# Expert weights kept on chip in the tail of a convolution, attention and expert kernel, with token numbers in buffers of their own

## The chip, the cores and the metric

The kernel runs on one core of a Trainium2 chip. The metric is the device time of one execution in microseconds (us); less is better. A profiled execution gives the trace from which all the rows below are taken.

A core has five engines that run side by side, each through its own instructions in order: TensorE (PE, with its weight loads as PEld), VectorE (DVE), ScalarE (ACT), GpSimd (POOL) and SyncE (SP). SP and POOL mostly start DMA transfers here; sixteen DMA engines carry them out.

## The reference, cut to what matters

```python
# layer 0: 32 convolution paths (1x1, 3x3, 1x1, each with batch norm and relu), summed
x = relu(paths.sum(axis=0) + x)                       # (8, 56, 56, 256)
# layer 1: attention without softmax, then a mixture of experts
t = to_tokens(x)                                      # 8 images of 3136 tokens of 256 numbers
t = t + attention(layernorm(t))                       # per head: q (k^T v) / N, plus its input
tokens = layernorm(t)
probs = softmax(tokens @ router_w.T)                  # 8 experts
rw, re = top_k(probs, 2); rw = rw / rw.sum()
out = tokens
for e in range(8):
    h = gelu(tokens @ w1[e] + b1[e])
    out = out + combine[:, e:e + 1] * (h @ w2[e] + b2[e])
t = t + out
```

Each token goes through two experts only: its first choice and its second choice. All is in 32-bit floating point.

## The kernel before

The tokens of the 8 images form 56 chunks of 448 tokens (7 per image). The main loop (L1542) runs over 65 slots. In a slot the convolution of one chunk is worked on beside the attention of the chunk eight slots back, the routing of earlier chunks, and a number of expert tiles. The convolution's last slot is 56. Slots 57 to 64 have attention (chunks 49 to 55), routing and expert tiles; after the loop, L1604 issues the expert tiles that are left. "The tail" below is everything from slot 57 on.

**Routing.** For a chunk, VectorE works out both choices of each token and its place in the expert's list. POOL then scatters each token's row (256 numbers, two weights, the token's number) into a table in memory, `regions[0]` for first choices and `regions[1]` for second choices: eight indirect DMAs per chunk (`scatter`, L1162). When a round of chunks is closed (`closing`, L548; in the last image after its chunks 1, 3, 5 and 6), `plan_steps` (L1189) makes a table on the chip that lists full tiles of 256 rows: for each tile its first row and its expert. The tiles of a round are numbered first choices before second choices. There are 210 tiles in all. The last round holds tiles 176 to 209; 30 of these start in rows that belong partly to other tiles (`low` is not None), and of such a tile only the rows from `low` on are added.

**One tile.** `take_rows` (L1350) reads the tile's first row into a register of SP and starts the load of 256 rows (259 KB) into `z`, one of 8 buffers. `take_weights` (L1361) reads the expert's number into a register of SP and starts the load of that expert's weights (513 KB) from `Wd`, a table in memory, into `w`, one of 4 buffers. `tile_in` (L1369) transposes the rows on TensorE (`te`), ScalarE copies them to `eT`. `tile_mid` multiplies by the first matrix (`ph`, L1415), ScalarE applies gelu (`hT`, L1419). `tile_out` multiplies by the second (`py`, L1431 and L1435), ScalarE scales by the token's weight into `y` (L1439), one of 4 buffers. `tile_add` (L1444) lets POOL add `y` to the rows of the output in memory: two indirect DMAs per tile (L1453), each for 128 tokens, whose token numbers are read from `z` itself, or for the partial tiles from a small tile `index` that VectorE makes (L1386 and L1387).

**Order.** In block n (`moe_steps`, L1473) stand, one after the other: `tile_in(n)`, first half of `tile_mid(n-1)`, second half and `take_rows(n+2)`, first half of `tile_out(n-2)` and `take_weights(n+1)`, second half of `tile_out(n-2)`. With the first two goes a `tile_add`. Slots 57 to 64 get 45 such blocks; the rest follows after the loop. The order on TensorE, ScalarE and VectorE is written out by hand, with places in the slot (`places`); SP's and POOL's instructions are ordered by the framework. The list `apart` is filled in slot 57 (L1599); from then on the two halves of `ph` and of `py` have separate PSUM banks.

**Waits around the change.** A row buffer is free for a later tile when its last reader is done: the scaling on ScalarE (the weights stand in `z`), and, where the token numbers are read from `z`, the scatter-add's landing. A `y` buffer is free when the scatter-adds of that tile have landed. `ordered_sum` (L1461) lets each scatter-add of a (round, choice) group wait until all those of the group before have landed, because a token has one row in each group. The row loads of a round wait for all `regions` scatters and for the writes of the output's base values by chunk (`out_dram<-X`, L1034) of that round (`before`, in `entry`, L1325).

Of the kernel before, what the change touches and what calls it, by code (L numbers as in the profile page):

```python
# [8 lines left out]
F32 = mybir.dt.float32  # L9
BF16 = mybir.dt.bfloat16  # L10
I32 = mybir.dt.int32
# [14 lines left out]
def kernel(  # L26
# [24 lines left out]
    nc = tc.nc  # L51
    B, N, C = x.shape
# [3 lines left out]
    E = w1.shape[0]  # L56
    HC = 32
    NH = C // HC
    P = 128
# [32 lines left out]
            tc.add_manual_dep(ins, halved[0].name, SYNC, reason="not needed by the first chunk")  # L92
        xs_in[s] = X

    xtp = ctx.enter_context(tc.tile_pool(name="xtp", bufs=4))
    taps = ctx.enter_context(tc.tile_pool(name="taps", bufs=1))
    split = ctx.enter_context(tc.tile_pool(name="split", bufs=1))
    hlp = ctx.enter_context(tc.tile_pool(name="hlp", bufs=2))
    setup_pool = tc.tile_pool(name="setup", bufs=1)
    setup = setup_pool.__enter__()  # L100

# [9 lines left out]
    for g in range(NG):  # L111
        nc.scalar.dma_start(
            out=bn2s[32 * g : 32 * g + 32],
            in_=bn2[32 * g : 32 * g + 32].rearrange("(a e) k -> e a k", a=4),
# [117 lines left out]
    for dx in range(3):  # L232
        for g in range(NG):
            nc.gpsimd.dma_start(
                out=W2s[dx : 3 * 32 : 3, g],
                in_=W2[32 * g : 32 * g + 32].rearrange(
                    "q (dy dx o) -> dx q dy o", dy=3, dx=3
                )[dx],
# [218 lines left out]
    slots = ctx.enter_context(tc.tile_pool(name="slots", bufs=4))  # L457
# [43 lines left out]
    ROW = C + 3  # L501
    WROW = 2 * NF * C + NF
# [5 lines left out]
    def paced(ins):  # L508

        tc.add_manual_dep(ins, pace[0].name, SYNC, reason="spread over the slot")  # L510
        return ins
# [17 lines left out]
    Wd = tc.dram_tile([E, P, WROW], F32, name="Wd")  # L529
# [44 lines left out]
    for e in range(M):  # L574
# [5 lines left out]
        out=below, in_=below, compare_op=ALU.is_ge, fill=0.0, base=-1,  # L580
# [8 lines left out]
        out=earlier, in_=earlier, compare_op=ALU.is_ge, fill=0.0, base=-1,  # L589
# [14 lines left out]
    def unordered(ins, group, keep=()):  # L604

        tc.declare_no_dep(ins, group=group, keep=keep, reason="other rows")
# [715 lines left out]
    got, weights_of, turned, hidden, ready = {}, {}, {}, {}, []  # L1322
    landed = set()

    def entry(i, j, most):  # L1325

        place, own, k, partial, b = slot_of[i]
        loads, (value,) = nc.values_load_multi_w_load_instructions(
            place[0:1, j : j + 1], engines=[mybir.EngineType.SP],
            min_val=0, max_val=most,  # L1330
            skip_runtime_bounds_check_because="a tile's row and expert, made on the chip",
        )
        if b not in landed:
            landed.add(b)
            for ins in before[b]:
                tc.add_manual_dep(loads[0].ins, ins.name, SYNC, reason="rows of the tiles")
        return value

    def empty_rows(e):
        pad = slots.tile([P, 2, ROW], F32, tag="rows", name=f"pad_{e}", bufs=8)  # L1340
        nc.gpsimd.memset(pad, 0.0)
        for k in range(2):
            ins = nc.sync.dma_start(
                out=regions[k][e * CAPR : e * CAPR + TR, :].rearrange("(h p) c -> p h c", p=P),
                in_=pad,
            ).ins
            paced(ins)
            filled(0, ins)

    def take_rows(i):  # L1350
        row = entry(i, 0, E * CAPR - TR)
        z = slots.tile([P, 2, ROW], F32, tag="rows", name=f"rows_{i}", bufs=8)
        region = regions[slot_of[i][2]]
        ins = nc.sync.dma_start(
            out=z, in_=region[bass.ds(row, TR), :].rearrange("(h p) c -> p h c", p=P)
        ).ins
        unordered(ins, "rows")
        tc.add_to_no_dep_group("tiles", ins)
        got[i] = z

    def take_weights(i):  # L1361
        e = entry(i, 1, E - 1)
        w = slots.tile([P, WROW], F32, tag="w", name=f"w_{i}")
        nc.sync.dma_start(
            out=w, in_=Wd[bass.ds(e, 1), :, :].rearrange("e p c -> (e p) c")
        )
        weights_of[i] = w

    def tile_in(i):  # L1369
        z = got.pop(i)  # L1370
        k = slot_of[i][2]
        tp = ps_mm.tile([P, NF, TR], F32, tag="mm", name=f"te_{i}")
        for f in range(NF):
            for h in range(2):
                nc.tensor.transpose(  # L1375
                    tp[:, f, h * P : (h + 1) * P], z[:, h, f * P : (f + 1) * P], ident
                )
        eT = work.tile([P, NF, TR], F32, tag="eT", name=f"eT_{i}")
        nc.scalar.copy(eT, tp)
        g = z[:, :, C + k]  # L1380
        index = [z[:, h, C + 2 :].bitcast(I32) for h in range(2)]
        low = slot_of[i][3]
        if low is not None:
            index = slots.tile([P, 2], I32, tag="index", name=f"index_{i}", bufs=12)
            past = slots.tile([P, 2], I32, tag="past", name=f"past_{i}", bufs=2)
            nc.vector.tensor_scalar(past, pos, low, float(1 << 30), ALU.is_lt, ALU.mult)  # L1386
            nc.vector.tensor_tensor(  # L1387
                index, z[:, :, C + 2].bitcast(I32), past, ALU.bitwise_or
            )
            index = [index[:, h : h + 1] for h in range(2)]  # L1390
        turned[i] = (eT, g, index)

    apart = []
# [29 lines left out]
    def tile_out(i, h):  # L1423
# [15 lines left out]
        nc.scalar.activation(y[:, h, :], ps, AF.Identity, scale=g[:, h : h + 1])  # L1439
        ready.append((i, h))  # L1440

    blocks = {}

    def tile_add():  # L1444
# [97 lines left out]
    for s in range(S + A + 1):  # L1542
        a = s - A
        work_of = []
        era = " alone" if s < A else ""
        if s <= S:
            work_of.append((0.0, 1.0 if is_chunk(s) else 0.1, conv3_steps(s)))
        if is_chunk(s + 2):
            work_of.extend(at("conv1" + era, conv1_steps(s + 2)))
        if is_chunk(s + 1):  # L1550
            work_of.extend(at("taps" + era, [(0.0, lambda: spread_taps(s + 1))]))
            work_of.extend(at("conv2" + era, conv2_steps(s + 1)))
        if is_chunk(s - 1):
            if s < S:
                work_of.extend(at("end" + era, end_steps(s - 1)))
            else:
                work_of.append((0.12, 0.99, end_steps(s - 1)))
        if is_chunk(a + 1):
            work_of.extend(at("fetch", [(0.0, lambda: fetch(a + 1))]))
        if is_chunk(a):  # L1560
            opens = a % NCH == 0
            if opens:
                work_of.extend(at("image", image_steps(a // NCH)))
            if a + A > S:
                work_of.extend(at("attention first last" if opens else "attention last", attn_steps(a)))
            else:
                work_of.extend(at("attention first" if opens else "attention", attn_steps(a)))
        work_of.extend(left)
        left = []
        group = waiting  # L1570
        if waiting and put_off(waiting[0]):
            group = [] if waiting[0] == a - 1 else waiting[:1]
        if group and (len(group) == 2 or group[-1] % NCH == NCH - 1):
            last_image = group[-1] >= S - NCH
            compute, scatters = route_steps(group)
            rt = places["route" if s < S else "route last"]
            work_of.append((rt[0], rt[1], compute))
            if last_image:
                work_of.append((places["scatter last"][0], 0.995, sum(scatters, [])))
            else:  # L1580
                work_of.append((places["scatter"][0], 0.995, scatters[0]))
                left = [(0.0, places["scatter"][1], steps) for steps in scatters[1:]]
            if group[-1] in closing:
                work_of.append((places["plan"][0], places["plan"][1], plan_steps(closing.index(group[-1]))))
            waiting = waiting[len(group) :]
        while r + 1 < len(closing) and known_in[r + 1] <= s:
            r += 1
        if r >= 0 and r + 1 < len(closing):
            goal = upto + (known_after[r] - 2 - upto) // (known_in[r + 1] - s)
            if r + 2 < len(closing):  # L1590
                goal = min(known_after[r] - 2, goal if s < known_in[1] else tiles_by(s))
            work_of.append((places["tiles"][s <= known_in[r]], places["tiles"][2], moe_steps(upto, goal)))
            upto = goal
        if s == 1:
            center_router()
        if 1 <= s <= E:
            work_of.append((0.5, 0.5, [(0.0, lambda: copy_weights(s - 1))]))
            work_of.append((0.8, 0.8, [(0.0, lambda: empty_rows(s - 1))]))
        if s == S + 1:  # L1599
            apart.append(s)  # L1600
        issue(*work_of)
        if is_chunk(a):
            waiting.append(a)
# [60 lines left out]
```

## Time and profile before

| | |
|---|---|
| time, median of 3 runs | 3093.45 us (3087.57 to 3095.67) |
| time of the profiled execution | 3092.02 us |
| its span in the trace | 3090.3 us |
| PE busy | 2875.4 us (93%) |
| DVE busy | 2124.4 us (69%) |
| ACT busy | 1920.2 us (62%) |
| POOL busy | 1800.1 us (58%) |
| loads `w<-Wd` | 210, 513.0 KB each |
| loads `rows<-regions` | 210, 259.0 KB each |
| scatter-adds of `y` (L1453) | 420, in two forms (token numbers from `rows` or from `index`) |

"Busy" is the time in which the engine had an instruction under way; DMA-issuing instructions count only for POOL's indirect DMAs. The rows of the trace read: start, duration, engine, line, operation, output `<-` inputs, shapes; in square brackets how long the engine was idle before and what by the trace released it. Where an instruction waits for several things, the trace names the one that came last by its own account, which can be one that had long been done. In the page's strip of forty slices, the last eight cover the tail and the two slots before it:

```profile
PE   7999898888999999999999999999999997997798
DVE  6877778788777777787777777787778784544000
POOL 2332344445465765756766666576664556676677
DMA  3534344436456777677776776767766666998897
```

Each digit is the busy share of a slice of 77 us in tenths. VectorE has little to do in the tail, POOL and the DMA engines more than before.

### The profile page before, as it was taken

The numbers are of one execution on the slowest core, as the hardware profiler recorded it, in microseconds if no ns is written. First come the engines' busy times: TensorE is split into PE (matmuls) and PEld (weight loads), VectorE is DVE, ScalarE is ACT, GpSimd is POOL, SyncE is SP. The second block draws the span as 40 slices with busy tenths as digits, with TensorE's granted clock in tenths as the row PEclk, the third lists the DMA queues.
The fourth block names the chain that finished last, engine by engine and source line by source line (L and its number), as shares of the span: only waits on it lengthen the run. The fifth ranks groups of instructions, "written<-read, shape, count | busy, mean of one in ns | idle before, by whom it ended". The sixth has DMA issues, their size and how long they took to land.

```text
span 3090.3 us, 53454 instructions
## 1 busy us (share of the span) xinstructions
PE 2875.4 (93%) x16677; PEld 1645.2 (53%) x16677; DVE 2124.4 (69%) x5532; ACT 1920.2 (62%) x3859; POOL 1800.1 (58%) x1333
## 2 busy tenths in 40 slices
PE   7999898888999999999999999999999997997798
PEld 3334443433455555555555555555555554776687
DVE  6877778788777777787777777787778784544000
ACT  4666566556666666667766666666666764554355
POOL 2332344445465765756766666576664556676677
PEclk8999999889999999999999999999999999998899
DMA  3534344436456777677776776767766666998897
GB/s 101 151 118 129 115 141 134 129 98 198 140 158 185 186 193 188 177 198 190 193 193 164 197 197 171 200 168 199 198 171 175 184 169 157 228 254 201 201 236 172
DMA packets 321708, 537.53 MB, mean 174 GB/s; under 512 B 40192, under 2 KB 231824, under 8 KB 321424
## 3 DMA queue, kind: packets, MB, share of 16 engines
q1 hardware_dynamic: 238464, 429.89, 45.6%
q0 software_dynamic: 82368, 103.47, 18.6%
q8 instruction: 133, 2.18, 0.3%
q14 instruction: 151, 1.24, 0.1%
q10 hardware_dynamic: 592, 0.76, 0.1%
HBM read 248.01 MB, written 192.55 MB: 143 GB/s over the span
## 4 chain that ended last, share of the span: by engine, by line
PE 72%; DVE 8%; ACT 6%; POOL 5%; DMA 5%; issue 4%; SPq 0%; ACTq 0%; POOLq 0%; DVEq 0%
PE c L660 14%; PE su L681 13%; PE ph L1415 11%; PE py L1435 9%; PE at L983 7%; PE kv L829 3%; PE c L324 3%; ACT r L665 3%; POOL hsd L793 3%; PE te L1375 3%; PE c L288 2%; DVE r L668 2%; PE py L1431 2%; DMA w<-Wd 2%; DMA out_dram<-y,rows 2%
## 5 line engine op out<-in xcount | busy, mean ns | idle before, releaser
L668 DVE SCALAR_TENSOR_TENSOR r<-c,nb,r 128x448 f32<-128x448 f32 x1792 | 1128.3, 677 | 401.2 <-ACT r L665 395.5
L665 ACT ACTIVATE r<-c,b3t 128x448 f32<-128x448 f32 x1792 | 1036.6, 634 | 342.6 <-PE c L660 338.1
L1453 POOL DMA_INDIRECT out_dram<-y,rows x360 | 567.0, 1575 | 415.6 <-ACT y L1439 262.8
L660 PE MATMUL c<-hl,W3hl 64*128 64x448 f32 x3584 | 684.9, 427 | 32.5 <-ACT r L665 18.7
L1163 POOL DMA_INDIRECT regions<-pay,rrowi x448 | 428.5, 957 | 308.9 <-PE c L660 172.8
L660 PEld LDWEIGHTS c<-hl,W3hl 64*128 64x128 f32 x3584 | 324.3, 188 | 490.6 <-issue 207.7
L681 PE MATMUL su<-r,gather 128*32 128x448 f32 x3584 | 532.2, 564 | 36.3 <-DVE r L668 32.5
L1415 PE MATMUL ph<-eT,w 128*128 128x256 f32 x1680 | 454.5, 402 | 40.2 <-DMA w<-Wd 24.0
L1439 ACT ACTIVATE y<-py,rows 128x256 f32<-128x256 f32 x420 | 196.9, 473 | 442.0 <-PE py L1435 364.9
L1435 PE MATMUL py<-w,hT 128*128 128x256 f32 x1680 | 432.8, 382 | 0.0
L1415 PEld LDWEIGHTS ph<-eT,w 128*128 128x128 f32 x1680 | 301.2, 194 | 173.0 <-issue 45.8
L793 POOL TENSOR_TENSOR hsd<-hsd,half 112x36 f32<-112x36 f32 x49 | 302.7, 6178 | 88.0 <-DVE hsd L791 84.1
L754 POOL TENSOR_TENSOR norm<-t,hmean 112x512 f32<-112x512 f32 x112 | 115.5, 1057 | 361.0 <-DVE hmean L743 220.9
L1419 ACT ACTIVATE hT<-ph,w 128x256 f32<-128x256 f32 x420 | 198.1, 476 | 187.7 <-PE ph L1415 130.9
L1435 PEld LDWEIGHTS py<-w,hT 128*128 128x128 f32 x1680 | 292.1, 192 | 29.3
L983 PE MATMUL at<-tab,tT 128*112 128x272 f32 x896 | 258.2, 411 | 7.1 <-ACT r L665 5.9
L681 PEld LDWEIGHTS su<-r,gather 128*32 128x32 f32 x3584 | 97.2, 109 | 218.7 <-issue 101.7
L1431 PE MATMUL py<-b2hl,own 128*128 128x256 f32 x420 | 182.2, 434 | 11.6 <-ACT lg L991 7.8
L983 PEld LDWEIGHTS at<-tab,tT 128*112 128x112 f32 x896 | 148.3, 179 | 81.5 <-issue 27.7
L987 DVE SCALAR_TENSOR_TENSOR X<-at,rs,X 112x256 f32<-112x256 f32 x224 | 107.0, 478 | 107.2 <-PE at L983 106.6
L1431 PEld LDWEIGHTS py<-b2hl,own 128*128 128x128 f32 x420 | 80.5, 192 | 141.8 <-issue 48.0
L324 PE MATMUL c<-R,W2t 96*32 96x448 f32 x1344 | 149.3, 546 | 0.1
(263 smaller groups left out, 3063.1 us busy)
## 6 DMA issues: line engine op xcount, KB each, us to landing
w<-Wd SPq DMA_DIRECT2D x210, 513.0 KB
rows<-regions SPq DMA_DIRECT2D x210, 259.0 KB
xi<-in_x_dram SPq DMA_DIRECT2D x56, 448.0 KB
hl<-hi SPq DMA_DIRECT2D x112, 224.0 KB
tTs<-xT SPq DMA_DIRECT2D x56, 448.0 KB
ts<-t SPq DMA_DIRECT2D x56, 448.0 KB
tT<-tTs SPq DMA_DIRECT2D x56, 448.0 KB
X<-ts SPq DMA_DIRECT2D x56, 448.0 KB
```

The lines of the kernel that those rows point to most:

```text
L324: nc.tensor.matmul(ps[0][32 * g : 32 * g + 32, :CH], W2t[:, g, dy, :], R[:, g, :].rearrange("q (r w) -> q r w", w=W58)[:, dy : dy + ROWS, ...
L660: product = nc.tensor.matmul(tiles[g][:, :CH], W3hl[rows, ab, cg, :], hl[rows, ab, :], start=True, stop=True)
L665: nc.scalar.activation(r, tiles[0][:, :CH], AF.Relu, bias=b3t[:, cg, 2 * ab : 2 * ab + 1])
L668: nc.vector.scalar_tensor_tensor(r, tiles[1][:, :CH], nb3[:, cg, 2 * ab + 1 : 2 * ab + 2], r, op0=ALU.max, op1=ALU.add,)
L681: nc.tensor.matmul(ps[32 * c4 : 32 * c4 + 32, :CH], gather, unit.pop((s, 4 * u + c4)), start=(ab == 0), stop=(ab == NQ - 1),)
L793: nc.gpsimd.tensor_tensor(sd, sd, half[:T, :].rearrange("q (k h) -> q k h", k=KT), ALU.pow)
L983: nc.tensor.matmul(ps, tT[:, f, k * T : (k + 1) * T], tables_of[b][:, f, :], start=(f == 0), stop=(f == NF - 1),)
L1163: ins = nc.gpsimd.indirect_dma_start(out=regions[n], out_offset=bass.IndirectOffsetOnAxis(ap=v["row_i"][:, (m - group[0]) * KT + k, n : n ...
L1415: nc.tensor.matmul(ps, w[:, f * C + hf * P : f * C + (hf + 1) * P], eT[:, f, :], start=(f == 0), stop=(f == NF - 1),)
L1431: nc.tensor.matmul(ps, own.to_broadcast([P, P]), b2hl, start=True, stop=False)
L1435: nc.tensor.matmul(ps, hT[:, f, h * P : (h + 1) * P], w[:, (NF + f) * C : (NF + f + 1) * C], start=False, stop=(f == NF - 1),)
L1453: ins = nc.gpsimd.indirect_dma_start(out=out_rows, out_offset=at, in_=y[:, h, :], in_offset=None, compute_op=ALU.add, **partial,).ins
```

## The change

The convolution's four pools of buffers move to the other side of the on-chip memory and are closed at slot 57. In their place one tile `experts` (128 partitions, 8 experts, 1026 numbers each) is made there, and one DMA on SP's queue loads all weights into it. From slot 57 on, `take_weights` no longer loads from memory: VectorE reads the expert's number into a register and copies that expert's part of `experts` into `w`. Also from slot 57 on, the token numbers of the tiles that are not partial are copied by VectorE into an `index` tile; there are 20 such tiles instead of 12. The row buffers are 7 instead of 8, from the start of the kernel.

```diff
-    xtp = ctx.enter_context(tc.tile_pool(name="xtp", bufs=4))
-    taps = ctx.enter_context(tc.tile_pool(name="taps", bufs=1))
-    split = ctx.enter_context(tc.tile_pool(name="split", bufs=1))
-    hlp = ctx.enter_context(tc.tile_pool(name="hlp", bufs=2))
+    conv_pools = [
+        tc.tile_pool(name=name, bufs=bufs, side="right")
+        for name, bufs in (("xtp", 4), ("taps", 1), ("split", 1), ("hlp", 2))
+    ]
+    xtp, taps, split, hlp = (p.__enter__() for p in conv_pools)
...
-    def entry(i, j, most):
+    def entry(i, j, most, engine=mybir.EngineType.SP):
...
-            place[0:1, j : j + 1], engines=[mybir.EngineType.SP],
+            place[0:1, j : j + 1], engines=[engine],
...
-        if b not in landed:
+        if b not in landed and engine == mybir.EngineType.SP:
...
-        z = slots.tile([P, 2, ROW], F32, tag="rows", name=f"rows_{i}", bufs=8)
+        z = slots.tile([P, 2, ROW], F32, tag="rows", name=f"rows_{i}", bufs=7)
...
     def take_weights(i):
+        w = slots.tile([P, WROW], F32, tag="w", name=f"w_{i}")
+        if apart:
+            e = entry(i, 1, E - 1, mybir.EngineType.DVE)
+            nc.vector.tensor_copy(
+                w, experts[0][:, bass.ds(e, 1), :].rearrange("q e c -> q (e c)")
+            )
+            weights_of[i] = w
+            return
         e = entry(i, 1, E - 1)
-        w = slots.tile([P, WROW], F32, tag="w", name=f"w_{i}")
...
-        if low is not None:
-            index = slots.tile([P, 2], I32, tag="index", name=f"index_{i}", bufs=12)
+        if apart and low is None:
+            index = slots.tile([P, 2], I32, tag="index", name=f"index_{i}", bufs=20)
+            nc.vector.tensor_copy(index, z[:, :, C + 2].bitcast(I32))
+            index = [index[:, h : h + 1] for h in range(2)]
+        elif low is not None:
+            index = slots.tile([P, 2], I32, tag="index", name=f"index_{i}", bufs=20)
...
         if s == S + 1:
+            for pool in reversed(conv_pools):
+                pool.__exit__(None, None, None)
+            stay = ctx.enter_context(tc.tile_pool(name="stay", bufs=1, side="right"))
+            experts.append(stay.tile([P, E, WROW], F32, name="experts"))
+            nc.sync.dma_start(out=experts[0], in_=Wd.rearrange("e p c -> p e c"))
             apart.append(s)
```

More of the change, by code (lines that the diff above doesn't have):

```diff
@@ L1339, in empty_rows @@
     def empty_rows(e):
-        pad = slots.tile([P, 2, ROW], F32, tag="rows", name=f"pad_{e}", bufs=8)
+        pad = slots.tile([P, 2, ROW], F32, tag="rows", name=f"pad_{e}", bufs=7)
         nc.gpsimd.memset(pad, 0.0)
@@ L1440, in tile_out @@
         ready.append((i, h))
+    experts = []
     blocks = {}
```

## Prediction

> **What bounds the kernel now.** I read the table by stretches first, because the change acts only in the last slots of the loop. The columns are the stretch, its length, busy time of PE, PEld, DVE, ACT and POOL with instruction counts, the granted clock, the DMA share and GB/s.
>
> ```profile
> 2641.00:2697.00 56.00, 53.47 (x284) 45.91 (x283) 29.78 (x134) 29.72 (x71) 36.33 (x27) 0.97 0.97 243
> 2697.00:2887.00 190.00, 157.24 (x792) 133.70 (x791) 75.91 (x347) 90.75 (x217) 138.74 (x111) 0.91 0.87 224
> 2887.00:2955.00 68.00, 59.17 (x287) 49.87 (x286) 1.69 (x10) 29.86 (x66) 41.37 (x28) 0.95 0.89 205
> 2955.00:3090.00 135.00, 122.59 (x647) 107.85 (x646) 8.21 (x49) 72.03 (x148) 104.47 (x68) 0.97 0.82 202
> ```
>
> TensorE looks like the bound and the DMA engines nearly full. The waits of the tail (from 2450 us, engines and SP's queue) seem to confirm that weights and row buffers come late:
>
> ```profile
> ACT y L1439 <- DMA out_dram<-y,rows: 54.8, 13, 12.2
> PE ph L1415 <- DMA w<-Wd: 24.0, 16, 3.6
> PE te L1375 <- DMA rows<-regions: 8.6, 4, 7.5
> SPq L1354 <- DMA out_dram<-y,rows: 163.0, 42, 13.4
> SPq L1364 <- PE py L1435: 121.6, 45, 10.0
> ```
>
> The largest engine wait of these is not for weights: ScalarE waits to write `y` until an older scatter-add of `y` has landed. So I read POOL's instructions in order of time. POOL issues two scatter-adds per tile (L1453) and eight `regions` scatters per chunk (L1163):
>
> ```profile
> 2744.25 1.55 POOL L1453 DMA_INDIRECT out_dram<-y,rows  x1 [0.30 <-ACT X L1025]
> 2746.10 1.55 POOL L1453 DMA_INDIRECT out_dram<-y,rows  x1 [0.30 <-issue]
> 2754.82 1.54 POOL L1453 DMA_INDIRECT out_dram<-y,rows  x1 [7.17 <-DMA out_dram<-X]
> 2908.20 1.54 POOL L1453 DMA_INDIRECT out_dram<-y,rows  x1 [0.30 <-issue]
> 2915.90 1.54 POOL L1453 DMA_INDIRECT out_dram<-y,rows  x1 [6.16 <-ACT hT L1419]
> 3015.50 1.54 POOL L1453 DMA_INDIRECT out_dram<-y,index  x1 [0.30 <-issue]
> 3021.39 1.56 POOL L1453 DMA_INDIRECT out_dram<-y,rows  x1 [4.34 <-ACT y L1439]
> ```
>
> One scatter-add takes 1.55 plus 0.30, so 1.85 us, or 3.70 per tile; one `regions` scatter 0.94 plus 0.30, so 1.25. From 2696 to the last scatter at 3083.22 POOL has no gap above 0.8 us except eight. They fall just at `ordered_sum`'s borders (L1461): the first scatter of one (round, choice) group waits until the whole group before has landed. Counting back from tile 209, the gaps stand before tiles 144, 149, 154, 165, 168, 172, 176 and 193, which are group borders; the borders at 158 and 162 are covered by `regions` scatters. The releasers named in brackets had long been done. Start to start, the eight are 8.72, 7.69, 6.90, 5.34, 7.70, 6.16, 6.57 and 5.89 us: 54.97 us, of which 8 x 1.85 would pass anyway. The borders cost 40.2 us.
>
> So POOL's queue carries the tail. TensorE runs ahead until the four `y` buffers stop it, and its waits for `w` lie inside that lead. In the last stretch both are close: TensorE needs 4.13 us per tile (one group of eight `ph` matmuls to the next in the chain: 3037.46 to 3041.59), POOL 3.70. Only from 2641 to 2697 is POOL waiting for tiles, and there TensorE has 53.5 busy of 56 us and no wait for `w`.
>
> **What the skill says.** The Trainium skill, "SBUF — State Buffer", section "Who interferes with whom": a VectorE copy in a two-port mode and a GpSimd instruction exclude each other, the later one blocks. "VectorE: DVE Perf Modes", section "What auto-detection actually checks": a single-source instruction with both sides in SBUF gets such a mode. The new weight copy is one. The trace agrees only in part. `hi` (L340, 128x448, 394 ns) is such a copy by its speed; it met a scatter-add already running at 961, 1298 and 2417 us, and these took 1.61 to 1.62 us instead of 1.54 to 1.60, while `hi` itself took 0.59 once. But an instruction with two SBUF inputs that had begun 0.16 us ahead of POOL's held it up for 0.5 us:
>
> ```profile
> 2856.49 0.76 DVE L1270 TENSOR_TENSOR big<-iot,qi 128x578 f32<-128x578 f32 x1
> 2856.65 2.07 POOL L1453 DMA_INDIRECT out_dram<-y,rows  x1 [0.30 <-issue]
> ```
>
> "DMA: Bandwidth & Descriptors", section "Queues, rings and completion order": each DMA engine takes turns between the queues that have packets. So scatter packets share engines with the weight packets. The landing times of L1453 agree: median 5.4 us from 2690 to 3090, and 2.7 from 3066 on, once the loads have stopped:
>
> ```profile
> DMA to landing us min/median/max: 2.7/5.4/8.9
> DMA to landing us min/median/max: 2.7/2.7/2.7
> ```
>
> **The change part by part.**
>
> *Weight loads leave SP and the DMA engines.* From slot 57 (about 2641 us, the first tile whose halves have banks of their own) 81 tiles follow, so some 81 loads of 513 KB go: 41.6 MB. In the stretch 2697 to 2887 SP issues 29 of them, 15.2 MB of 42.6 MB (224 GB/s x 190 us), so 36% of the bytes; where only tiles run it is half (513 KB beside 259 of rows and 256 of scatter-adds). The 24.0 us of `ph` waiting for `w` go as well, but they lie in TensorE's lead over POOL: late next is the scatter-add's landing that frees `y`, and behind it POOL. I count them at nothing. If POOL were not the cover they would be worth 24 us.
>
> *Faster landings.* At the eight borders POOL waits for a landing and nothing else. Of their mean interval of 6.87 us I take 0.9 for the restart (an estimate, the trace does not part the two), so the landing is 6.0, inside the 2.7 to 8.9 of the view. The floor is 2.7. With 36 to 50% of the bytes away I let half of the excess of 3.3 go: 1.65 us each, 13.2 us in all. Bounds: 0 if scatter packets hinder themselves, 26 if landings reach the floor.
>
> *A VectorE copy per tile.* 128x1026 elements. From `hi`: 394 ns for 448; at two elements a cycle of 0.96 GHz (the skill's clock, page "VectorE: DVE Perf Modes") 233 ns of it is streaming, 160 fixed, so 1026 take 0.69 us; at one element a cycle 1.23. Ahead of it stands one load of the expert's number into a register: SP's L1328 shows 278 ns, while the skill ("DMA: Bandwidth & Descriptors", "Latency and other measured facts") gives a floor near 600 ns; I take 0.3 to 0.6. With the index copy (0.16, as L1387) VectorE gets some 1.4 us per tile, 63 us for the 45 tiles of slots 57 to 64, in which it is busy 107 of 314 us. There is room. The copy waits for the buffer that tile n-3 leaves, one block back in TensorE's order, and behind it stand attention's VectorE operations, which need later matmuls anyway; who waits for those is ScalarE's normalisation and then POOL's `regions`, which lag. Cost in VectorE time: none.
>
> *The copy against POOL.* POOL starts an instruction every 1.85 us. A copy of 0.69 us in progress at such a start delays it by what is left of it, less 0.09 (the 0.76 us instruction above had 0.60 left and cost 0.52). With random phase that is 0.60 x 0.60 / (2 x 1.85), so 0.097 us per tile. Between tile 137 and 175 POOL is the bound: 39 x 0.097, 3.8 us lost. Behind that TensorE's 4.13 against 3.70 takes it up. Bounds: 0, and, if the phase is locked badly, 0.6 a tile.
>
> *The index copy and seven row buffers.* With its own index buffer a row tile is free after ScalarE has scaled `y`, no longer after the scatter has landed. SP's 163 us at L1354 mostly go. This takes no work from POOL, so by itself nothing; what is late next is `y`, which still waits for the scatter. Seven instead of eight row buffers act earlier too, before slot 57: there SP waited at L1354 only 5.1 us (168.1 in the whole run, 163.0 after 2450), since a tile takes 6 us or more; 0 to 2 us, taken as 0.
>
> *The load of all weights.* 4.2 MB on SP's queue, after the last reader of the convolution's tiles (the last load into `tTs` is issued at 2584.93, its transposes follow). At the 243 GB/s of the next stretch it needs 17 us, and later loads queue behind it. Between 2600 and 2641 it is covered by the tiles of slot 56; if it were issued only at 2641, the first copies would wait up to 10 us for it, in the stretch where POOL has no backlog. I take 0, range 0 to 10.
>
> Sum: -13.2 + 3.8 = -9.4 us. The span of 3090.3 becomes 3080.9, and the profiled run of 3092.02 becomes 3082.6. That run lies 1.4 below the median of 3093.45; from the median I forecast 3084.
>
> **The rivals.**
>
> *POOL bound, gain kept* (the forecast): 3070 to 3092. For it: a POOL queue without gaps but at borders. Chance 0.50.
>
> *The gain is eaten:* the load of all weights is late (+10), or landings hardly shorten because rows, attention and the scatters themselves fill the engines (saving 0 to 4). Time 3092. For it: windows with a DMA share of 0.60 (700 to 1000 us) still show a median landing of 4.6. Chance 0.20.
>
> *Weights are the bound after all,* as the chain of waits suggests, which names `w<-Wd` again and again between 2727 and 2971: then the waits of `ph` (24.0) and `te` (8.6) both go, 33 us, giving 3061. Against it: ScalarE stood at `y`, not at `hT`, for the longer time. Chance 0.09.
>
> *Slower:* the copy holds POOL's starts. Place: every tile from 137 on, 73 tiles. Price: up to 0.6 us a tile when the phase is locked (the copy is released by matmuls that wait for `y`, which waits for a scatter). It decides from 13.2/73, so 0.18 us a tile. With 0.45 it is 33 us against 13 saved: 3113. Chance 0.21.
>
> **How the numbers follow.** A change under 0.3% (9.3 us) cannot be told from none here. Of the forecast's 0.50 some 0.38 lie beyond that, 0.12 within. Faster: 0.38 + 0.09 = 0.47. Same: 0.12 + 0.18 = 0.30. Slower: 0.02 + 0.21 = 0.23. The forecast's own range is 3070 to 3092; the range for all goes from 3064 (near the floor of landings) to 3108 (0.38 us a tile).
>
> **What would show it.** Right: POOL's order still without gaps in the tail, its eight border intervals near 5.2 us; landings of L1453 near 4; no `w` wait at `ph`, yet ScalarE still waiting for `y`; scatter-adds of up to 2.1 us now and then. Wrong: POOL idle for want of `y`, so that TensorE sets the end; scatter-adds at 1.9 us in the mean; TensorE standing still near 2650 for the weights' load; or another order of POOL's scatters that uncovers the borders at 158 and 162 or covers others.

## The result and the profile after

The changed kernel takes 3102.02 us (median of 7 runs, 3097.27 to 3105.78), the kernel before 3095.67 in the runs beside it (3086.28 to 3101.12). The ratio is 1.0024, with a 95% interval of 1.0014 to 1.0033: slower by a quarter of a per cent. The interval leaves out "no change", though the step is smaller than the 0.3% named in the prediction. The profiled execution took 3103.07 us, its span is 3101.2, so 10.9 more than the 3090.3 of the profile before.

The table by stretches of the changed kernel, with the columns of the prediction's first table:

```profile
2641.00:2697.00 56.00, 50.65 (x264) 43.13 (x265) 33.73 (x139) 26.92 (x64) 34.86 (x26) 0.97 0.74 152
2697.00:2887.00 190.00, 160.86 (x821) 136.58 (x820) 92.91 (x398) 90.77 (x224) 141.26 (x108) 0.92 0.70 145
2887.00:2955.00 68.00, 56.62 (x270) 45.91 (x269) 21.81 (x61) 25.92 (x64) 47.85 (x31) 0.95 0.64 103
2955.00:3101.00 146.00, 124.78 (x655) 109.02 (x653) 27.02 (x79) 62.72 (x151) 113.12 (x69) 0.94 0.51 84
```

The last two columns, the share of the DMA engines and the GB/s, fell as they should: 0.87 to 0.70 and 224 to 145 between 2697 and 2887. The scatter-adds' packets land sooner too. Their time to landing from 2690 on (minimum, median, maximum), where before the median was 5.4:

```profile
DMA to landing us min/median/max: 2.7/3.8/5.7
```

So the change did to the transfers what it says, and the kernel is slower all the same. The waits from 2450 on, of the engines and of SP's queue:

```profile
ACT y L1451 <- DMA out_dram<-y,index: 162.1, 51, 12.4
DVE w L1366 <- PE py L1447: 147.1, 42, 12.8
SPq L1355 <- ACT y L1451: 244.9, 66, 10.6
```

No wait of `ph` for `w` is left (24.0 us before), and SP's row loads now wait for ScalarE's scaling, not for landed scatters. ScalarE's wait for a landed scatter-add before it writes `y` has grown to 162.1 us, from 56.9 in both forms (54.8 and 2.1). POOL carries the tail more than before, so the next thing to read is POOL's order of time, here in the last stretch:

```profile
2991.03 1.54 POOL L1466 DMA_INDIRECT out_dram<-y,index  x1 [0.30 <-ACT hT L1431]
2992.88 1.97 POOL L1466 DMA_INDIRECT out_dram<-y,index  x1 [0.30 <-issue]
2995.16 1.54 POOL L1466 DMA_INDIRECT out_dram<-y,index  x1 [0.30 <-ACT eT L1387]
2997.01 1.97 POOL L1466 DMA_INDIRECT out_dram<-y,index  x1 [0.30 <-issue]
2999.29 1.54 POOL L1466 DMA_INDIRECT out_dram<-y,index  x1 [0.30 <-ACT y L1451]
3001.14 1.98 POOL L1466 DMA_INDIRECT out_dram<-y,index  x1 [0.30 <-issue]
```

Every second scatter-add takes 1.97 instead of 1.54 us. VectorE's order of the same microseconds shows what goes with it:

```profile
2992.75 0.70 DVE L1366 COPY w<-experts 128x1026 f32 x1 [3.10 <-PE py L1447]
2996.87 0.70 DVE L1366 COPY w<-experts 128x1026 f32 x1 [3.10 <-PE py L1447]
3001.00 0.70 DVE L1366 COPY w<-experts 128x1026 f32 x1 [3.10 <-PE py L1447]
```

Each weight copy starts some 0.14 us before a scatter-add, and that scatter-add is 0.43 us longer. The phase is locked: the two keep the same distance from tile to tile, and the numbers fit one reason for it. TensorE releases the copies, and it runs here at its own 4.13 us per tile: between 2970 and 3055 its matmuls wait 0.2 us in all. POOL by itself would need 3.70 per tile, so its starts move up on the copies by 0.43 us a tile. But the earlier in a copy a scatter-add begins, the longer it is held. The two settle where the hold is just 4.13 - 3.70 = 0.43 us. Of the 15 tiles 184 to 198, 12 pay 0.43 or 0.44 us, and the 15 together 6.1. At tile 199 the copy comes 0.02 us after the scatter-add's start, doesn't hold it, and the lock is lost. As long as it lasts, POOL, the faster of the two, is bound to TensorE's pace and no longer works off what it is behind. The run without index copies, below, locks again at the same price: 0.43 or 0.44 us for each of the tiles 183 to 192 and 198 to 204. The waits between 2970 and 3065 say the same. Before the change:

```profile
ACT y L1439 <- PE py L1435: 22.0, 44, 0.5
ACT y L1439 <- DMA out_dram<-y,index: 1.3, 1, 1.3
```

and after it:

```profile
ACT y L1451 <- DMA out_dram<-y,index: 41.1, 20, 3.9
```

Before, ScalarE waited there for TensorE, since POOL had caught up; now it waits for landed scatters to write `y`. TensorE's last `te` is at 3069.88 before and at 3071.55 after, so TensorE lost 1.7 us over the whole run; the last scatter-add ends 14.9 us behind it before and 24.1 us after.

An account of POOL's queue, summed from the trace, runs from the first scatter-add of tile 135 to the end of the last one. In each kernel it is 150 scatter-adds and 56 `regions` scatters, 345.1 us at 1.54 and 0.94 us with 0.30 between them. "Lengthening" is what the instructions take above 1.54 or 0.94; "borders" is what POOL stands idle above 0.30 before the group borders. The last column is the time from the first routing matmul (`rk`) of slot 57 to tile 135's first scatter-add. Ratios are to the kernel before, with 95% intervals; the seven variants are those of the experiments below.

| kernel | ratio | POOL in all | lengthening | borders | slot 57 |
|---|---|---|---|---|---|
| before | 1 | 390.5 | 3.3 | 40.2 | 53.5 |
| before, a second profile | | 388.5 | 2.8 | 39.1 | 53.3 |
| after | 1.0024 (1.0014 to 1.0033) | 398.1 | 18.6 | 33.4 | 56.2 |
| copy issued twice | 1.0053 (1.0039 to 1.0068) | 401.0 | 24.4 | 28.9 | 59.1 |
| without index copies | 1.0018 (1.0011 to 1.0026) | 393.6 | 18.7 | 28.8 | 56.2 |
| index copies alone | 0.9979 (0.9971 to 0.9987) | 384.6 | 2.8 | 35.1 | 53.4 |
| weights by a reduction | 0.9972 (0.9960 to 0.9983) | 378.2 | 1.8 | 29.6 | 57.2 |
| the same, five `y` buffers | 0.9974 (0.9964 to 0.9984) | 378.6 | 2.0 | 30.0 | 57.1 |
| the same, from slot 58 on | 0.9960 (0.9946 to 0.9974) | 381.0 | 2.6 | 31.5 | 53.3 |
| weights copied by ScalarE | 0.9953 (0.9939 to 0.9966) | 377.1 | 2.1 | 27.5 | 53.4 |

From before to after: lengthening +15.3, borders -6.8, the rest -0.8, so +7.7 on POOL; slot 57 +2.7; arrival at slot 57 +0.6. That is the 10.9 us of the two spans. The last of these is no effect of the change that I can name: in the ten profiles the first `rk` matmul of slot 57 starts anywhere from 2636 to 2647 us, without an order that follows the edits. The earliest, at 2636.09, is that of the run without index copies, whose profiled execution was the fastest of 19; so the account, which leaves the arrival out, is compared below, and not the spans.

Where slot 57 lost its 2.7 us is seen best beside the kernel before. TensorE's, ScalarE's and VectorE's order of time before:

```profile
2672.69 0.15 DVE L1011 SCALAR_TENSOR_TENSOR nm<-mv,rs 112x4 f32<-112x4 f32 x1
2672.88 0.60 ACT L1018 ACTIVATE pay<-X,nm,rs 112x256 f32<-112x256 f32 x1 [2.38 <-DVE nm L1011]
2677.18 0.57 ACT L1379 COPY eT<-te 128x512 f32<-128x512 f32 x1
2677.80 1.99 PE L1415 MATMUL ph<-eT,w 128*128 128x256 f32 x8 [1.36 <-ACT eT L1379]
2679.63 1.08 PE L983 MATMUL at<-tab,tT 128*112 128x272 f32 x4
```

and after:

```profile
2674.29 0.16 DVE L1012 SCALAR_TENSOR_TENSOR nm<-mv,rs 112x4 f32<-112x4 f32 x1
2674.48 0.60 ACT L1019 ACTIVATE pay<-X,nm,rs 112x256 f32<-112x256 f32 x1 [3.15 <-DVE nm L1012]
2678.79 0.56 ACT L1387 COPY eT<-te 128x512 f32<-128x512 f32 x1
2679.40 2.44 PE L1427 MATMUL ph<-eT,w 128*128 128x256 f32 x8 [2.12 <-ACT eT L1387]
2681.63 2.02 PE L984 MATMUL at<-tab,tT 128*112 128x272 f32 x4
```

Counted from the slot's first `rk` matmul (2640.78 and 2641.39), `nm` is 1.0 us later: VectorE had a weight copy of 0.70 us (at 2666.52) and an index copy in the chain of small operations that ends there. ScalarE waits for `nm`, `eT` stands behind its normalisations in order, `ph` waits for `eT`. That is 1.0 of the 2.7. The rest is in durations: eight `ph` matmuls take 2.44 us instead of 1.99, four `at` matmuls 2.02 instead of 1.08, and the first `py` matmuls behind them are slower too. TensorE's granted clock explains it: it reads 0.50 from 2680.8 to 2684.2, where it is 1.00 at the same place of the kernel before. The last section comes back to it.

### The profile page after: what moved, and what is told of

It reads as the page before. It is cut to its first block, busy times and chain, and to the rows that moved or that the text cites. A ratio compares the mean times of both kernels' runs of the same rounds, so it can differ in the third digit from the quotient of the medians.

```text
span 3101.2 us, 53478 instructions
## 1 busy us (share of the span) xinstructions
PE 2878.2 (93%) x16677; PEld 1643.4 (53%) x16677; DVE 2183.3 (70%) x5663; ACT 1906.4 (61%) x3859; POOL 1816.4 (59%) x1333
## 4 chain that ended last, share of the span: by engine, by line
PE 72%; DVE 8%; ACT 6%; POOL 6%; issue 5%; DMA 2%; ACTq 0%; DVEq 0%; POOLq 0%; SPq 0%
PE c L661 14%; PE su L682 13%; PE ph L1427 11%; PE py L1447 9%; PE at L984 7%; PE kv L830 3%; PE c L325 3%; ACT r L666 3%; POOL hsd L794 3%; PE te L1383 3%; PE c L289 2%; DVE r L669 2%; PE py L1443 2%; PE tu L729 1%; DMA out_dram<-y,index 1%
## 5 line engine op out<-in xcount | busy, mean ns | idle before, releaser
L1466 POOL DMA_INDIRECT out_dram<-y,rows x258 | 408.1, 1582 | 333.0 <-ACT y L1451 257.6
L1466 POOL DMA_INDIRECT out_dram<-y,index x162 | 264.1, 1630 | 95.9 <-ACT y L1451 44.1
L1366 DVE COPY w<-experts 128x1026 f32 x80 | 58.0, 725 | 173.5 <-PE py L1447 147.1
```

The source lines that it names most:

```text
L1466: ins = nc.gpsimd.indirect_dma_start(out=out_rows, out_offset=at, in_=y[:, h, :], in_offset=None, compute_op=ALU.add, **partial,).ins
```

## The experiments

**The weight copy as a reduction.** Same place, waits and bytes, another operation of VectorE: a sum over an axis of length one, which leaves the numbers as they are.

```diff
-            nc.vector.tensor_copy(
-                w, experts[0][:, bass.ds(e, 1), :].rearrange("q e c -> q (e c)")
+            nc.vector.tensor_reduce(
+                w, experts[0][:, bass.ds(e, 1), :].rearrange("q e (c o) -> q (e c) o", o=1),
+                AX.X, ALU.add,
             )
```

> The changed kernel with the weight copy written as a VectorE reduction over an axis of length one: same data, but an instruction that is not a copy in a two-port mode; I expect about 1.2 us instead of 0.70. Theory A (a copy in progress when POOL starts a scatter holds that start back; 15.3 us more of scatter durations than in the kernel before, 6.8 us less at the group borders, 3.3 us late at tile 135): the scatters' excess over 1.54 and 0.94 us from tile 135 on falls from 18.6 us to below 6, and the ratio to the kernel before falls from 1.0024 to 0.997 to 1.000. Theory B (VectorE's own time and order cost it, the longer copy more): ratio 1.003 to 1.005. Theory C (the token numbers' copies or the seven row buffers cost it): ratio stays at 1.0024.

Measured: 3085.42 us, ratio 0.9972 (0.9960 to 0.9983). The group of these reductions, then POOL's and VectorE's order of time:

```profile
L1366 DVE TENSOR_REDUCE w<-experts 128x1026 f32 x80 | 97.7, 1222 | 140.5 <-PE py L1448 102.4 <-ACT y L1452 25.1 <-issue 9.2
```

```profile
2991.04 1.54 POOL L1467 DMA_INDIRECT out_dram<-y,index  x1 [0.30 <-issue]
2992.89 1.54 POOL L1467 DMA_INDIRECT out_dram<-y,index  x1 [0.31 <-DVE index L1394]
2994.73 1.54 POOL L1467 DMA_INDIRECT out_dram<-y,index  x1 [0.30 <-issue]
```

```profile
2991.23 1.22 DVE L1366 TENSOR_REDUCE w<-experts 128x1026 f32 x1 [2.57 <-PE py L1448]
2995.36 1.22 DVE L1366 TENSOR_REDUCE w<-experts 128x1026 f32 x1 [2.81 <-PE py L1448]
```

The reduction is slower than the copy, 1.22 us against 0.70, and overlaps scatter-adds just so, yet none of these is longer than 1.54. Over the whole tail from tile 135, 36 scatter-adds began while a reduction was under way; they took 1.55 us in the mean. In the changed kernel 31 began while a copy was under way and took 1.88; 26 more, during which a copy began, took 1.66. So what costs is neither VectorE's time nor the extra access to memory, but this form of instruction beside POOL. POOL's account falls from 398.1 to 378.2 us; of that 16.8 is lengthening. The Trainium skill, "SBUF — State Buffer", section "Who interferes with whom", says that a `tensor_reduce` never contends with GpSimd on trn2; this run agrees.

**The copy issued twice.** The second copy writes the same numbers again.

```diff
+            nc.vector.tensor_copy(
+                w, experts[0][:, bass.ds(e, 1), :].rearrange("q e c -> q (e c)")
+            )
```

> The changed kernel with each weight copy issued twice. Theory A: twice the time in which a start of POOL can be held, so 10 to 15 us more of scatter durations and a ratio to the kernel before of 1.005 to 1.008. Theory B: VectorE has 0.7 us more per tile in its order, of which only slot 57's 3.3 us double: 1.003 to 1.004, with scatter durations as in the changed kernel. Theory C: stays at 1.0024.

Measured: 3110.56 us, ratio 1.0053 (1.0039 to 1.0068). POOL's order of time in the last stretch, and VectorE's:

```profile
2990.50 1.69 POOL L1469 DMA_INDIRECT out_dram<-y,index  x1 [0.30 <-ACT hT L1434]
2992.49 1.76 POOL L1469 DMA_INDIRECT out_dram<-y,index  x1 [0.30 <-issue]
2994.56 1.76 POOL L1469 DMA_INDIRECT out_dram<-y,index  x1 [0.30 <-ACT y L1454]
```

```profile
2991.41 0.70 DVE L1366 COPY w<-experts 128x1026 f32 x1 [2.30 <-PE py L1450]
2992.14 0.70 DVE L1369 COPY w<-experts 128x1026 f32 x1
```

Here both scatters of a tile are longer, by 0.15 to 0.22 us each: the first copy begins in the middle of one, the second is under way when the next begins. The lengthening grows from 18.6 to 24.4 us, a third, not twice, and less than the 10 to 15 us expected. In the last stretch it grows least (9.8 us for tiles 176 to 209, after 8.2): two scatter-adds of 1.76 with 0.30 each make 4.12 us, so POOL again keeps TensorE's pace, and the hold of 0.43 per tile is only shared out over two. That is what a lock on the slower engine's pace would do, and what a price per copy would not. The other loss is slot 57, at 59.1 us.

**The index copies.** First the change without them (weights copied on chip, seven row buffers, token numbers again read from `rows`). Then the index copies and the seven row buffers together, put into the kernel before, with its weight loads from memory. The core of both edits is this branch, taken out in the one, put in in the other:

```diff
-        if apart and low is None:
-            index = slots.tile([P, 2], I32, tag="index", name=f"index_{i}", bufs=20)
-            nc.vector.tensor_copy(index, z[:, :, C + 2].bitcast(I32))
-            index = [index[:, h : h + 1] for h in range(2)]
-        elif low is not None:
+        if low is not None:
```

> The changed kernel with the token numbers of whole tiles read from the row buffer again (no copy by VectorE, still seven row buffers), weights still copied. Theory A: POOL carries the tail and the weight copies remain, so the ratio stays within 1.001 to 1.004, though SP waits for landed scatters again. Theory C: ratio 1.000 or below. If freed row buffers were worth something behind the copies, it is slower than 1.004.

> The kernel before with the token numbers' copies and the seven row buffers alone; weights still come by DMA. Theory A: POOL's queue is as it was, SP's wait for landed scatters goes, ratio 0.999 to 1.001. Theory C: ratio 1.002 or above.

Measured: without them 3099.67 us, ratio 1.0018 (1.0011 to 1.0026); alone 3086.29 us, ratio 0.9979 (0.9971 to 0.9987). Without index copies the kernel is still slower than before, so the weight copies are enough for that; whether index copies help or harm beside them can't be told from these intervals. Alone (with the seven row buffers), the index copies make it faster, which none of the theories had expected. SP's waits from 2690 on without them:

```profile
SPq L1355 <- DMA out_dram<-y,rows: 230.3, 46, 14.7
```

In the kernel before this wait is 160.4 us over the same stretch; with the index copies alone the row loads no longer wait for a landed scatter at all, and what SP waits for longest is the weight loads' buffers:

```profile
SPq L1364 <- PE py L1439: 166.0, 62, 11.9
```

The lengthening of the index copies alone is 2.8 us, as before: these small copies of 0.16 us don't hold POOL up. Most of their gain is in the borders (35.1 us against 40.2 and 39.1). Why a border is shorter when rows can be loaded earlier, the traces don't show. The DMA engines are not less busy: their share between 2697 and 2887 is 0.93, against 0.87 before. This stays open.

**The copy on ScalarE.** Same on-chip weights, same index copies, the copy as a ScalarE instruction, and the expert's number read by ScalarE.

```diff
-            e = entry(i, 1, E - 1, mybir.EngineType.DVE)
-            nc.vector.tensor_copy(
+            e = entry(i, 1, E - 1, mybir.EngineType.Activation)
+            nc.scalar.copy(
```

> The changed kernel with the weight copy on ScalarE instead of VectorE. Theory A (VectorE's two-port copy holds POOL's starts): no such copy is left, the scatters' excess from tile 135 on is below 6 us as with the reduction (1.8), and tile 135 starts near 2694, since slot 57's chain on VectorE is free again; ScalarE gets about 1 us more per tile. Ratio to the kernel before 0.995 to 0.998. If weights kept on chip cost something of their own, it stays above 1.001.

Measured: 3079.79 us, ratio 0.9953 (0.9939 to 0.9966), faster than both kernels. It is the lowest median of all, though the next experiment's is within 0.5 us of it. The group of these copies, and the place in slot 57 that was shown above:

```profile
L1366 ACT COPY w<-experts 128x1026 f32 x80 | 84.3, 1054 | 4.7 <-issue 3.7 <-DVE X L988 0.3
```

```profile
2683.96 2.00 PE L1427 MATMUL ph<-eT,w 128*128 128x256 f32 x8 [1.54 <-ACT eT L1387]
2685.79 1.08 PE L984 MATMUL at<-tab,tT 128*112 128x272 f32 x4
```

A copy takes 1.05 us here, more than VectorE's 0.70, and costs nothing visible: POOL's lengthening is 2.1 us, slot 57 is back at 53.4 (though tile 135 starts at 2700.45 and not near 2694, since this profile reached slot 57 only at 2647.04), and ScalarE has room (119.84 busy of 190 us between 2697 and 2887). The border intervals have come down to 5.2 us in the mean, start to start, from 6.9. Against the reduction on VectorE the intervals of the two ratios (0.9939 to 0.9966, 0.9960 to 0.9983) overlap a little, so that ScalarE is the better place is likely, not settled.

**From slot 58 on.** The reduction again, but slot 57's tiles still load their weights from memory. This asks whether slot 57's 2.7 us come from VectorE's copies there.

```diff
-        if apart:
+        if len(apart) > 1:
...
             apart.append(s)
+        if s == S + 2:
+            apart.append(s)
```

> The kernel with the reduction, but copies only from slot 58 on; the tiles of slot 57 load their weights by DMA as before. If the late start of tile 135's scatter (2700.5 us with the reduction, 2694.3 before, 2697.6 with the copy) comes from VectorE's longer order in slot 57, it is back at 2692 to 2696 and the ratio falls from 0.9972 to about 0.995. If it comes from the load of all weights or from the fewer row buffers, tile 135 stays near 2700 and the ratio at 0.997.

Measured: 3080.20 us, ratio 0.9960 (0.9946 to 0.9974). From the first `rk` matmul to tile 135 it is 53.3 us again, and the wait for `eT` in slot 57 is 1.41 us, with the eight `ph` matmuls at 1.99. So the loss of slot 57 is VectorE's weight copies in that slot. That tile 135 would start as early as in the kernel before did not hold: it starts at 2698.64, since this profile reached slot 57 only at 2645.30. The slot's own length is the number to compare.

**Five `y` buffers.** The reduction, with `y` in five buffers instead of four; to make room, rows in six instead of seven. If TensorE's lead over POOL were what limits, this would help.

```diff
-            hidden[i].append(work.tile([P, 2, C], F32, tag="y", name=f"y_{i}", bufs=4))
+            hidden[i].append(work.tile([P, 2, C], F32, tag="y", name=f"y_{i}", bufs=5))
```

> The kernel with the reduction, with five y buffers instead of four and six row buffers instead of seven. If POOL's queue carries the tail, a longer lead of TensorE is worth nothing: ratio 0.996 to 0.9985, ScalarE's wait for y falls. If the y buffers themselves limit, it falls below 0.995.

Measured: 3084.61 us, ratio 0.9974 (0.9964 to 0.9984), beside 0.9972 with four. POOL's account is 378.6 and 378.2 us. ScalarE's wait for landed scatters fell, from 88.2 to 78.3 us, and that is worth nothing, as it must be when POOL's queue is the bound. The row buffer taken away at the same time could hide a small gain.

**The kernel before once more**, for a second profile of it, to see how far two profiles of one kernel differ.

> The kernel before, unchanged, profiled once more: how far two profiles of one program agree. The eight border intervals add up to 40.2 us above the plain cadence in the first profile; within 3 us of it, the 35.1 us of the kernel with the token numbers' copies alone is a difference; 5 us or more away, it is not readable from one profile.

Measured: one execution of 3091.29 us, span 3089.6. POOL's account is 388.5 instead of 390.5, borders 39.1 instead of 40.2, slot 57 53.3 instead of 53.5. So 2 us in the account are within what differs anyway; the 15.3 us of lengthening and the 2.7 of slot 57 are not.

## Why the prediction was wrong

The forecast was 3084 us, a gain of 9.4 us; measured is a loss of 6.4 between the medians and 10.9 between the profiles. 3102 lies inside the range given, but on the other side of the kernel before.

**POOL carries the tail: right.** There are no gaps in its queue from tile 135 on but at borders, a fifth `y` buffer brings nothing, and the 24.0 us of `ph` waiting for `w` went without a gain, as priced.

**Faster landings, -13.2 us: right in the median, half in the sum.** The median of 3.8 us is the forecast's "near 4". The eight border intervals came down from 6.87 to 6.10 us in the mean, not to 5.2, and the borders cost 33.4 instead of 40.2 us: 6.8 saved, not 13.2. Three of the eight in the changed kernel's order of POOL:

```profile
2828.64 1.55 POOL L1466 DMA_INDIRECT out_dram<-y,index  x1 [6.94 <-ACT y L1451]
2920.88 1.54 POOL L1466 DMA_INDIRECT out_dram<-y,index  x1 [3.11 <-ACT y L1451]
2960.00 1.54 POOL L1466 DMA_INDIRECT out_dram<-y,index  x1 [4.77 <-ACT y L1451]
```

The idle time in brackets went from 6.16 to 3.11 before tile 168 and from 5.03 to 4.77 before tile 176, but from 5.35 to 6.94 before tile 154. In the run with ScalarE's copies the mean interval is 5.2 and the cost 27.5 us, so 12.7 saved. It would be easy to say that held scatters keep the changed kernel's borders long, but two runs speak against it: without index copies the lengthening is as large (18.7 us) and the borders cost 28.8, and with the copy issued twice they cost 28.9 at 24.4 us of lengthening. Why the changed kernel saved only half stays open; each of these figures is of one profile. Nor is less traffic shown to be the whole reason where borders did shorten, since the index copies alone shorten them with more traffic.

**The copy's duration: right.** 0.69 us was worked out, 0.70 measured.

**The copy against POOL, +3.8 us: the step that failed.** Measured is 15.3 us of lengthening, 0.20 us for each of the 75 tiles. Three parts of the step were wrong:

- "With random phase": from tile 184 to 198 the phase is locked, and 12 of the 15 tiles pay 0.43 or 0.44 us where chance would have taken 0.097. That is 6.1 of the 15.3 us. The page on the state buffer and the row at 2856 us, where a scatter-add had been held 0.5 us by an instruction ahead of it, were read rightly for one meeting, but the number of meetings was taken from chance.
- "Behind that TensorE's 4.13 against 3.70 takes it up": tiles 176 to 209 were costed at nothing, and their scatter-adds lengthened by 7.9 us (8.2 after, 0.2 before). The difference of pace was no cover. It was how POOL worked off its backlog behind TensorE, and a lock takes just this difference away. From tile 176 to the end POOL takes 135.7 us instead of 130.3.
- Only scatters that begin during a copy were counted. Copies that begin during a scatter lengthen it too: 26 such scatter-adds hold 3.0 us above 1.54, and the 31 that began during a copy 10.4. The `regions` scatters add 3.1. For tiles 135 to 175, where 3.8 was forecast, scatter-adds and `regions` together lengthened by 7.3 with hardly any lock, about twice the forecast.

Undoing the holds, by the reduction, takes the ratio from 1.0024 to 0.9972, on the forecast's side. That its gain, 8.5 us between the medians, is near the forecast's 9.4 is in part luck: slot 57 lost 3.7 us there, and the index copies, priced at nothing, gain something by themselves.

**VectorE's time, "none": wrong in slot 57.** "behind it stand attention's VectorE operations, which need later matmuls anyway" left out slot 57. There POOL has no backlog, as the prediction itself said of this stretch, and VectorE's small operations stand on the path to ScalarE's `eT`. It cost 2.7 us, and 3.7 with the longer reduction.

**Index copies and seven row buffers, "by itself nothing": wrong, in the other direction.** Alone they gain 0.21% (0.13 to 0.29). The load of all weights at nothing: no wait for it is seen; it is issued at 2588.5, and the first copy starts at 2649.37, 0.75 us after the VectorE operation ahead of it.

**The rival "slower" named the mechanism and its place; its reason for the lock was another.** It thought of a loop, in which the copy waits for matmuls that wait for `y` and so for a scatter. In the last stretch TensorE waited for next to nothing (0.2 us); POOL came to TensorE's pace by being held. The rival's point of decision was 0.18 us per tile; measured is 0.20. It took 0.45 per tile for its time of 3113, near the 0.43 that a locked tile pays, but in tiles 135 to 175 only 8 of 41 pay over 0.3 us in their scatter-adds: there the lengthening is 7.3 us for 41 tiles, 0.18 each. Its weight against the forecast was too low, and the two paces, 4.13 and 3.70, with which the price of the lock could be worked out, both stood in the prediction.

## What to carry to other kernels

When instructions that come at a slower engine's pace can hold up a faster engine, don't price their meetings by chance. Where an earlier start means a longer hold, the faster can be held until it keeps the slower one's pace. The price per turn is then the whole difference of the two paces, and if the faster needed that difference to work off a backlog, the backlog stays to the end. Before moving work to the idlest engine by its busy share, look at what it shares with the engine that is the bound: here ScalarE's copy of 1.05 us was better than VectorE's of 0.70, whose form of instruction met POOL's.

## What the runs showed of the hardware

**How a copy and a scatter-add meet.** In the changed kernel's last stretch a copy of 0.70 us that began 0.06, 0.14, 0.20 and 0.26 us before a scatter-add made it 2.05, 1.97, 1.91 and 1.85 us long; 0.58 before, 1.59. So the scatter-add is held for what is left of the copy, less some 0.13 us. A copy that began 0.91 us into a scatter-add took its normal 0.70 and lengthened the scatter-add to 1.69; one at 0.57 took 0.97 and lengthened it to 1.63; one at 1.27 took 0.77 and did not lengthen it. Coming second can cost as much as coming first: earlier in the tail, copies that began 1.13 and 1.19 us into a scatter-add took 0.70 and made it 1.91 and 1.97. The Trainium skill's section "Who interferes with whom", named above, says of a copy in a two-port mode that whoever issues first has the shared ports for the whole instruction and the other fully blocks. The first case agrees but for 0.13 us. The second doesn't: from tile 135 on no copy took over 1.00 us, so one that came second was not kept waiting for the rest of the scatter-add.

**After a wait of about 2 us TensorE's clock can be halved.** In slot 57 `ph` waits for `eT` in all ten profiles. Where the wait was 1.36 to 1.56 us (before, twice; index copies alone; from slot 58 on; ScalarE), the eight matmuls took 1.99 to 2.00 us. Where it was 2.12, 2.17, 2.64, 2.67 and 2.93, they took 2.44, 2.59, 3.58, 3.47 and 3.78, and single matmuls 0.63 instead of 0.38. The granted clock in the traces says what the slowing is. In these five it falls to 0.50 for 3.4 us, and for 6.8 in the run with two copies; in the other five it is 1.00 there. The fall comes at its own time: in the changed kernel 1.4 us after the wait's end, with the first matmuls still at full speed, and in the kernel with the reduction 0.2 us before the wait is over. So a delay of 1 us ahead of such a point cost 2.7.

The Trainium skill, "TensorE: Matmul & The Clock Gate", section "Part 1: The HAM clock gate (the "warmup" mystery)", tells of such a slowing after an idle window of about 3.4 us, in windows that run on their own. The 3.4 us of halved clock agree, but a wait of 2.1 us was enough. The length of one wait doesn't decide alone: at the first `rk` of slot 57 a wait of 1.79 us was followed by a halved clock (from slot 58 on), and waits of 1.82 and 1.83 were not (index copies alone, without index copies). At what length it sets in, these runs don't show.
